# Last token group: row tables kept in the ring's tiles, token rows loaded between weights, and the experts' second bias added by VectorE

## The chip, the cores and the metric

The kernel runs on one core of a Trainium2 chip. The metric is the device time of one execution in microseconds (us). The kernel before was run three times: 3078.43, 3081.97 and 3084.2 us, median 3081.97. One more execution was taken with the hardware profiler; it took 3079.39 us.

Names of engines: PE is TensorE (PEld its weight loads), DVE is VectorE, ACT is ScalarE, POOL is GpSimd, SP is SyncE, which here only issues DMAs. SPq and POOLq are DMAs issued by those two.

## What is computed

One layer on a graph of 6250 nodes with 256 features and 206250 edges, sorted by destination, followed by a mixture of experts. Cut to what matters:

```
xn = layernorm(x)
# 1. attention over each node's edges, 8 heads of 32
sim  = (q[dst] * k[src]).sum(per head) / sqrt(32);  attn = softmax over the edges of one dst
agg  = segment_sum(attn * v[src], dst) @ Wo.T + bo
# 2. linear attention over all nodes, 8 heads of 64, with normalised k and v
mix  = (q @ (k.T @ v) / N) @ w_out.T + b_out
x    = x + agg + mix
# 3. mixture of experts: 8 experts, capacity C = ceil(1.25 * 6250 / 8)
h    = layernorm(x)
p    = softmax(h @ gate_w + gate_b);  idx = argmax(p)
buf[idx, pos] = h                      # pos: the token's place among those of its expert
y    = relu(buf[e] @ w1[e] + b1[e]) @ w2[e] + b2[e]
x    = x + y[idx, pos] * p[idx]        # dropped tokens (pos >= C) add nothing
```

All of it is in float32.

## The kernel before

**Blocks and groups.** The 6250 nodes make 49 blocks of 128 rows, one row in each partition of the on-chip memory. The nodes are ordered by their number of edges inside three groups of blocks, `GROUPS = (20, 17, 12)`, so that one block's nodes have nearly the same number of edges.

**Foreground: attention.** For each block the kernel runs over its edges in chunks of five, `W = 5`. POOL issues one indirect DMA per edge slot (L615) that gathers 128 key and value rows of 2 KB into a tile `kvg` of a ring of `RING = 11` tiles (pool `kvp`). For each chunk DVE multiplies the keys by the queries (L1353) and sums per head (L1354). When a unit (a block, or a part of one, some six chunks) has all its sums, ACT takes the exponentials, and during the next unit DVE multiplies the values by them (L1305) and PE adds them up with an identity matmul (L1309, into the PSUM tile `pa`). At the end of a unit DVE scales the sum into `ag` (L1327) and POOL scatters it to `agg_tab` (L823). POOL gathers at most `LEAD = 2` chunks ahead; a ring tile comes free when PE has read it at L1309.

**Background: everything else.** The order of all instructions is written out by the code, and each engine works through its own in that order. The other stages are Python generators. `background(n)` runs them for `n` units of estimated work, at two places within each chunk of attention: before `weigh` (L1305, L1309) and between `weigh` and the keys' products (L1353, L1354). So one chunk reads: a piece of background, L1305 and L1309, a piece of background, L1353 and L1354. When all blocks of group g have been scattered, the generator `behind(g)` is queued. It runs, in order:

- `output_stage`: for each block, load the aggregate, x transposed and x (L856, L199, L864), transpose the aggregate (L870, copied by ACT at L871), multiply by `weff` (L879) and `wo` (L888), add the two output biases by a matmul of `ones_d` and `bsum` (L891), add x (L897, L900), normalise (L902 to L916), write the sum to the DRAM table `x2_tab` (L917) and the normalised rows to `h_tab` (L918), and compute the gate's logits. Its steps s1 to s7 are pipelined over blocks.
- `routing`: the expert of each token, its place, the rows `row_to` and `row_from`, and the expert of each tile `tile_e`, on DVE.
- `to_tiles`: read `h_tab` again (L1087) and scatter the rows to `xbuf`, sorted by expert (L823).
- `experts`: tiles of 256 tokens in groups 0 and 1 (17 and 16 tiles), of 128 tokens in group 2 (19 tiles). Phase (0, t) is the first matmul of tile t (`hidden`, L1167, with relu on ACT at L1173), phase (1, t) the second (`final`, L1184, once per 128 tokens). Each phase loads one weight block of 1.0 to 1.2 MB, chosen by `tile_e` (L1132). The second bias is row 0 of a block of zeros behind the second weights: `final` adds it by a matmul with ones (L1188), ACT copies the result out of PSUM (L1190), SP writes it to `ybuf` (L1192). Token rows come in at L1142; that load waits for all scatters of its group.
- `finish`: gather each token's row from `ybuf` (L1227), read `x2_tab` (L1232), scale (L1244), add (L1248), write the output (L1249).

**The last group.** Groups 0 and 1 have the next group's attention to run beside. Group 2 has none: when its last aggregate is scattered, its stages run alone, from 2779 us to the end. Its weights go to the ring's tiles, which attention no longer needs, seven phases ahead (`AHEAD = 7`); the other groups have a pool of three tiles and load two ahead.

**SP's order.** SP issues its DMAs in the order of the code and stops at one whose wait isn't met. In the last group that order is: the output stage's loads and table writes, the reads of `h_tab` (each waits for a free buffer), seven weight loads, then the first two loads of token rows.

Of the kernel before, what the change touches and what calls it, by code (L numbers as in the profile page):

```python
# [9 lines left out]
F32 = mybir.dt.float32  # L10
# [3 lines left out]
ALU = mybir.AluOpType  # L14
# [4 lines left out]
P = 128  # L19
# [5 lines left out]
W = 5  # L25
RING = 11
LEAD = 2
PART = 44
GROUPS = (20, 17, 12)
# [39 lines left out]
def gps_layer(  # L69
# [59 lines left out]
    def rows(b):  # L129
        return tail if b == NB - 1 else P  # L130
# [21 lines left out]
    with tc.manual_schedule():  # L152
# [31 lines left out]
        bad = keep.tile([P, 3], F32, name="bad")  # L184
        flag_i = keep.tile([1, 1], I32, name="flag_i")
        bsum = keep.tile([P, D], F32, name="bsum")
        weff = keep.tile([P, DC, D], F32, name="weff")
        rstd = keep.tile([P, NB], F32, name="rstd")
        finite = keep.tile([P, NB], F32, name="finite")
# [494 lines left out]
        def linear_attention():  # L684
# [26 lines left out]
                )  # L711
                yield 2.4

            nc.vector.tensor_add(bsum, bias[:, 0, :], bias[:, 1, :])
            nc.vector.tensor_scalar(bsum, bsum, float(D) / P, None, op0=ALU.mult)
            wmf = wm.rearrange("p c g d -> p c (g d)")
            for c0 in range(0, 2 * MI, 512):
                less_mean(wmf[:, :, c0 : c0 + 512], 512)
# [127 lines left out]
        def output_stage(gi, logits):  # L846
# [2 lines left out]
            d2, d3 = late_pools["d2"], late_pools["d3"]  # L849
            wo, gw, gb = (late_pools[k] for k in ("wo", "gw", "gb"))  # L850
            T = {}

            def load(i):
                b = b0 + i
                ag = d2.tile([P, D], F32, name="in0")
                ld = nc.sync.dma_start(ag, agg_tab[b * P : (b + 1) * P, :])  # L856
                for s in sent["agg", gi]:
                    tc.add_manual_dep(ld.ins, s.ins.name, sync_data, reason="rows of any block")
                xT = d2.tile([P, D], F32, name="in1").rearrange("p (c q) -> p c q", c=DC)
                x_transposed(xT.rearrange("p c q -> p (c q)"), b)  # L860
                xb = d3.tile([P, D], F32, name="row_a")
                if rows(b) < P:
                    nc.vector.memset(xb, 0.0)
                nc.sync.dma_start(xb[: rows(b)], x[b * P : b * P + rows(b), :])  # L864
                T[i] = dict(ag=ag, xT=xT, xb=xb)

            def turn(t, to):
# [16 lines left out]
            def s2(i):  # L884
                t = T[i]
                po = t["po"]
                for c in range(DC):
                    nc.tensor.matmul(  # L888
                        po[:, 1, :], t["agT"][:, c, :], wo[:, c, :], start=False, stop=False, skip_group_check=True
                    )  # L890
                nc.tensor.matmul(po[:, 1, :], ones_d, bsum, start=False, stop=True, skip_group_check=True)  # L891

            def s3(i):
                t = T[i]
                x2 = d3.tile([P, D], F32, name="row_b")
                t["x2"] = x2
                nc.vector.scalar_tensor_tensor(  # L897
                    x2, t["po"][:, 0, :], rstd[:, b0 + i : b0 + i + 1], t["xb"], op0=ALU.mult, op1=ALU.add
                )
                nc.vector.tensor_add(x2, x2, t["po"][:, 1, :])  # L900
                st = d2.tile([P, 6], F32, name="std")
                nc.vector.bn_stats(st, x2)  # L902
                t["mv"] = d3.tile([P, 2], F32, name="mvd")
                nc.vector.bn_aggr(t["mv"], st)
                t["rs"] = d3.tile([P, 2], F32, name="rsd")
                nc.scalar.activation(t["rs"][:, 0:1], t["mv"][:, 1:2], AF.Sqrt, bias=eps)

            def s4(i):
                t = T[i]
                b = b0 + i  # L910
                rs = t["rs"]
                nc.vector.reciprocal(rs[:, 0:1], rs[:, 0:1])
                nc.vector.tensor_scalar(rs[:, 1:2], t["mv"][:, 0:1], rs[:, 0:1], -1.0, op0=ALU.mult, op1=ALU.mult)
                h = d3.tile([P, D], F32, name="hd")
                t["h"] = h
                nc.scalar.activation(h, t["x2"], AF.Identity, bias=rs[:, 1:2], scale=rs[:, 0:1])  # L916
                nc.sync.dma_start(x2_tab[b * P : (b + 1) * P, :], t["x2"])  # L917
                nc.sync.dma_start(h_tab[b * P : (b + 1) * P, :], h)  # L918

            def s5(i):  # L920
                t = T[i]
# [156 lines left out]
        def to_tiles(gi):  # L1078
            b0, ng = FIRST_OF[gi], GROUPS[gi]
            d3 = late_pools["d3"]  # L1080
            hs = {}

            def load(i):
                if i < ng:
                    b = b0 + i
                    hs[i] = d3.tile([P, D], F32, name="row_a")
                    nc.sync.dma_start(hs[i], h_tab[b * P : (b + 1) * P, :])  # L1087

            load(0)
            load(1)  # L1090
            yield 2.5
            for i in range(ng):
                load(i + 2)
                spaced_scatter(
                    ("x", gi), out=xbufs[gi][:, :],
                    out_offset=bass.IndirectOffsetOnAxis(ap=row_to[:, b0 + i : b0 + i + 1], axis=0),
                    in_=hs.pop(i), in_offset=None,
                )
                if i % 2:
                    yield 2.5  # L1100

        def experts(gi):
# [9 lines left out]
            for t in range(1, n_t):  # L1112
                phases += [(0, t), (1, t - 1)]
            phases.append((1, n_t - 1))
            AHEAD = 7 if last else 2

            def load_w(i):
                if i >= len(phases):
# [58 lines left out]
            def final(t, k, part):  # L1177
                w2_t = T[t][1]
                w = w2_t[:, :V2].rearrange("p (f d) -> p f d", f=FC)
                if part == 0:  # L1180
                    T[t]["py"] = bank((D,))
                py = T[t]["py"]
                for f in range(part * FC // 2, (part + 1) * FC // 2):
                    nc.tensor.matmul(  # L1184
                        py, T[t]["hT"][:, f, k * P : (k + 1) * P], w[:, f, :], start=(f == 0), stop=False
                    )
                if part == 1:
                    nc.tensor.matmul(py, ones[:, :P], w2_t[:, V2 : V2 + D], start=False, stop=True)  # L1188
                    yr = d2.tile([P, D], F32, name="res")
                    nc.scalar.copy(yr, py)  # L1190
                    r0 = t * size + k * P
                    nc.sync.dma_start(ybufs[gi][r0 : r0 + P, :], yr)  # L1192

            for i in range(AHEAD):
                load_w(i)
            load_x(0)
            load_x(1)
            yield 2.0
            turn(0)
            yield 1.0  # L1200
# [17 lines left out]
        def finish(gi):  # L1218
# [4 lines left out]
            def load(i):  # L1223
                if i < ng:
                    b = b0 + i
                    y = d3.tile([P, D], F32, name="row_a")
                    nc.gpsimd.indirect_dma_start(  # L1227
                        out=y, out_offset=None, in_=ybufs[gi][:, :],
                        in_offset=bass.IndirectOffsetOnAxis(ap=row_from[:, b : b + 1], axis=0),
                    )  # L1230
                    x2 = d3.tile([P, D], F32, name="row_b")
                    nc.sync.dma_start(x2, x2_tab[b * P : (b + 1) * P, :])  # L1232
                    T[i] = y, x2

            load(0)
# [706 lines left out]
```

## Time and profile before

| what | value |
|---|---|
| median of three runs | 3081.97 us |
| the profiled execution | 3079.39 us |
| its span, first to last instruction | 3077.6 us |
| PE busy | 2209.4 us, 72% |
| DVE busy | 2027.4 us, 66% |
| POOL busy | 1921.5 us, 62% |
| ACT busy | 640.9 us, 21% |
| DMA | 730.27 MB, mean 237 GB/s |
| gathers on POOL (L615) | 1715, the last at 2750.2 us |
| second matmuls, bias matmuls (L1188) | 85 tiles of 128 rows, two passes each |
| first and last bias matmul (L1188), groups 0 and 1 / group 2 | 1485.1 and 2681.7 / 2899.8 and 3034.2 us |
| last aggregate scatter | 2778.65 us |

The span is the time between the first and the last instruction of the profiled execution. Busy shares are means over stages with different limits, so the stretches have to be read one by one. A line of the timeline gives the start in us, the duration in us, the engine, the line of the kernel, the operation, what is written from what is read, the shape, and how many equal instructions were merged; in brackets stands how long the engine was idle before it and what it then waited for. A float32 matmul runs in two passes, so each matmul of the code stands twice.

### The profile page before, as it was taken

Reading aid. Unit: us, or ns where it says so; the run is one execution under the profiler, and the core shown is the slowest. Engines: PE = TensorE matmul, PEld = TensorE weight load, DVE = VectorE, ACT = ScalarE, POOL = GpSimd, SP = SyncE. Lnnn points to the kernel's source line nnn. Section 1 sums busy time; section 2 is a strip of 40 time slices with the busy share of each in tenths; the row PEclk is TensorE's granted clock in tenths of the full one; section 3 lists DMA queues with packets and bytes.
Section 4 is the critical chain, followed back from the end, with each engine's and each line's share of the span. In section 5 each row is a group of like instructions: output and inputs, shape, how many; then the busy total and the mean of one; then the engine's idle time right before and its main releaser. Section 6 shows DMA issues by size and latency. Waiting matters only on the chain. (4 is left out here: it accounts for less than half of the span.)

```text
span 3077.6 us, 29537 instructions
## 1 busy us (share of the span) xinstructions
PE 2209.4 (72%) x9086; PEld 1722.8 (56%) x9086; DVE 2027.4 (66%) x2723; ACT 640.9 (21%) x1802; POOL 1921.5 (62%) x2114
## 2 busy tenths in 40 slices
PE   8845468777777655763989889455628999846494
PEld 3534345555555444652778777334527888735494
DVE  6468778888888867983767776565854767564000
ACT  5200013333333101210211111101202222112242
POOL 5435767777777777667777777776466767650101
PEclk9977689899998778886999999678869999978797
DMA  7755957677777668867888887767658988763783
GB/s 263 274 189 179 335 169 215 208 210 212 208 210 219 200 196 251 264 194 230 304 287 308 292 302 246 227 202 248 203 182 276 316 303 311 244 191 110 281 326 110
DMA packets 291641, 730.27 MB, mean 237 GB/s; under 512 B 46838, under 2 KB 152020, under 8 KB 278164
## 3 DMA queue, kind: packets, MB, share of 16 engines
q0 software_dynamic: 149744, 477.83, 50.0%
q1 hardware_dynamic: 141732, 250.47, 23.1%
q8 instruction: 75, 1.23, 0.2%
q14 instruction: 90, 0.74, 0.1%
HBM read 654.47 MB, written 73.64 MB: 237 GB/s over the span
## 5 line engine op out<-in xcount | busy, mean ns | idle before, releaser
L615 POOL DMA_INDIRECT kvg<-kv_tab,idx x1715 | 1625.8, 948 | 668.2 <-issue 430.1
L1309 PE MATMUL pa<-kvg,ident 128*128 128x256 f32 x3430 | 1012.1, 452 | 586.3 <-DVE kvg L1305 453.4
L1309 PEld LDWEIGHTS pa<-kvg,ident 128*128 128x128 f32 x3430 | 756.9, 227 | 826.3 <-DVE kvg L1305 543.0
L1353 DVE TENSOR_TENSOR kvg<-kvg,qc 128x1280 f32<-128x1280 f32 (+1 forms) x366 | 512.9, 1402 | 397.5 <-DMA kvg<-kv_tab,idx 322.0
L1354 DVE TENSOR_REDUCE sim<-kvg 128x40 f32<-128x1280 f32 (+1 forms) x366 | 513.3, 1402 | 12.6
L1305 DVE TENSOR_TENSOR kvg<-kvg,pr 128x1280 f32<-128x1280 f32 (+1 forms) x366 | 509.6, 1393 | 0.0
L1184 PE MATMUL bank<-wt,hTe 128*128 128x256 f32 x1056 | 246.9, 381 | 0.0
L1167 PE MATMUL bank<-xTe,wt 128*128 128x256 f32 x1056 | 242.6, 381 | 2.3 <-ACT xTe L1157 2.3
L1167 PEld LDWEIGHTS bank<-xTe,wt 128*128 128x128 f32 x1056 | 201.6, 191 | 30.5 <-ACT xTe L1157 3.0
L1184 PEld LDWEIGHTS bank<-wt,hTe 128*128 128x128 f32 x1056 | 200.9, 192 | 27.0
L1248 DVE TENSOR_TENSOR res<-bank,row_b 128x256 f32<-128x256 f32 x49 | 20.7, 422 | 279.9 <-ACT bank L1244 271.7
L731 PE MATMUL bank<-wm,xTm 128*128 128x512 f32 x392 | 177.6, 596 | 0.0
L1227 POOL DMA_INDIRECT row_a<-ybuf,row_from x49 | 46.4, 947 | 197.3 <-issue 189.3
L1173 ACT ACTIVATE hTe<-bank,wt 128x256 f32<-128x256 f32 x264 | 110.8, 471 | 262.2 <-PE bank L1167 262.2
L1190 ACT COPY res<-bank 128x256 f32<-128x256 f32 x85 | 31.7, 372 | 439.5 <-PE bank L1188 248.0
L731 PEld LDWEIGHTS bank<-wm,xTm 128*128 128x128 f32 x392 | 72.0, 193 | 71.2 <-issue 70.9
L823 POOL DMA_INDIRECT xbuf<-row_a,row_to x49 | 48.0, 980 | 95.0 <-DVE cmp L1068 66.3
L1281 ACT COPY qc<-qs 128x256 f32<-128x256 f32 x49 | 18.8, 383 | 414.5 <-DVE kvg L1353 312.5
L823 POOL DMA_INDIRECT agg_tab<-ag,node_ri x49 | 48.5, 990 | 84.2 <-DVE ag L1327 61.5
L1153 PE MATMUL bank<-ident,in 128*128 128x128 f32 x170 | 29.0, 286 | 99.9 <-DMA in<-xbuf 99.9
L760 ACT ACTIVATE ck<-bank,rk 128x64 f32<-128x64 f32 x392 | 86.1, 339 | 50.3 <-DVE rk L757 50.2
L524 PE MATMUL pkv<-wn,xT 128*128 128x512 f32 x196 | 90.9, 618 | 2.7 <-DVE kv L538 2.6
(254 smaller groups left out, 2202.2 us busy)
## 6 DMA issues: line engine op xcount, KB each, us to landing
wt<-in_w_rows_dram SPq DMA_DIRECT2D x33, 1152.0 KB, 7.6
wt<-in_w_rows_dram SPq DMA_DIRECT2D x33, 1028.0 KB, 5.4
kvg<-kv_tab,idx POOLq DMA_INDIRECT x1715, 3.9
kvg<-in_w_rows_dram SPq DMA_DIRECT2D x19, 1152.0 KB, 13.2
kvg<-in_w_rows_dram SPq DMA_DIRECT2D x19, 1028.0 KB
kv_tab<-kv SPq DMA_DIRECT2D x49, 256.0 KB, 3.0
xT<-in_xT_all_dram SPq DMA_DIRECT2D x24, 512.0 KB, 6.7
in<-xbuf SPq DMA_DIRECT2D x85, 128.0 KB, 8.9
```

What stands on the lines that cost most here:

```text
L524: nc.tensor.matmul(pkvs[b], xTs[b // GX][:, b % GX, c, :], wn[:, c, : 2 * D], start=(c == 0), stop=(c == DC - 1))
L615: nc.gpsimd.indirect_dma_start(out=kv[:, j - j0, :], out_offset=None, in_=kv_tab[:, :], in_offset=bass.IndirectOffsetOnAxis(ap=idx_of[b][: ...
L731: nc.tensor.matmul(pm, xT_of[b][:, c, :], wmf[:, c, s * MI : (s + 1) * MI], start=(c == 0), stop=(c == DC - 1),)
L760: nc.scalar.activation(cks[b][:, h, :], pms[b][0][:, h * MD : (h + 1) * MD], AF.Copy, scale=rk[:, h : h + 1])
L823: s = nc.gpsimd.indirect_dma_start(**kw)
L1167: nc.tensor.matmul(ph[:, k, :], w[:, c, f * P : (f + 1) * P], T[t]["xT"][:, c, :size], start=(k == 0 and c == 0), stop=(k == 1 and c == DC ...
L1173: nc.scalar.activation(T[t]["hT"][:, f, :size], ph[:, k, :], AF.Relu, bias=w1_t[:, V1 + f : V1 + f + 1])
L1184: nc.tensor.matmul(py, T[t]["hT"][:, f, k * P : (k + 1) * P], w[:, f, :], start=(f == 0), stop=False)
L1305: nc.vector.tensor_tensor(vals, vals, v["pr"][:, j0 - s0 : j1 - s0, :, None].to_broadcast([P, m, GH, GD]), ALU.mult)
L1309: nc.tensor.matmul(v["pa"], ident, kv[:, j, D:], start=(j0 + j == s0), stop=(j0 + j == s1 - 1),)
L1353: nc.vector.tensor_tensor(keys, keys, qc[:, None, :].to_broadcast([P, j1 - j0, D]), ALU.mult)
L1354: nc.vector.tensor_reduce(sim[:, j0 - s0 : j1 - s0, :], keys.rearrange("p j (h d) -> p j h d", d=GD), AX.X, ALU.add)
```

## The change

There are four edits.

1. In the last group, the normalised rows `h` and the sums `x2` stay on chip: four tiles of the ring, two for each, hold the twelve blocks. The writes to `h_tab` and `x2_tab` and the reads from them are left out for this group. With four tiles taken, `AHEAD` becomes 11 - 4 - 2 = 5.
2. In the last group, the two output biases are added to the x rows by POOL (`bias_all`) instead of by a matmul with `ones_d`.
3. In `experts`, two weight blocks are loaded, then the first two loads of token rows, then the other weights. For groups 0 and 1, which load two ahead, the order is as it was.
4. In all three groups, the second bias is written into all 128 rows of its block, and DVE adds it while it takes the result out of PSUM. The matmul with ones and ACT's copy go. The blocks keep their size.

```diff
--- before.py
+++ after.py
@@ -184,6 +184,7 @@
         bad = keep.tile([P, 3], F32, name="bad")
         flag_i = keep.tile([1, 1], I32, name="flag_i")
         bsum = keep.tile([P, D], F32, name="bsum")
+        bias_all = keep.tile([P, D], F32, name="bias_all")
         weff = keep.tile([P, DC, D], F32, name="weff")
         rstd = keep.tile([P, NB], F32, name="rstd")
         finite = keep.tile([P, NB], F32, name="finite")
@@ -711,8 +712,8 @@
                 )
                 yield 2.4
 
-            nc.vector.tensor_add(bsum, bias[:, 0, :], bias[:, 1, :])
-            nc.vector.tensor_scalar(bsum, bsum, float(D) / P, None, op0=ALU.mult)
+            nc.vector.tensor_add(bias_all, bias[:, 0, :], bias[:, 1, :])
+            nc.vector.tensor_scalar(bsum, bias_all, float(D) / P, None, op0=ALU.mult)
             wmf = wm.rearrange("p c g d -> p c (g d)")
             for c0 in range(0, 2 * MI, 512):
                 less_mean(wmf[:, :, c0 : c0 + 512], 512)
@@ -849,6 +850,14 @@
             d2, d3 = late_pools["d2"], late_pools["d3"]
             wo, gw, gb = (late_pools[k] for k in ("wo", "gw", "gb"))
             T = {}
+            last = gi == NG - 1
+            if last:
+
+                R = 2 * W
+                for name in ("h", "x2"):
+                    ts = [kvp.tile([P, W, 2 * D], F32, name="kvg") for _ in range(-(-ng // R))]
+                    ts = [t.rearrange("p j (k d) -> p (j k) d", k=2) for t in ts]
+                    late_pools[name] = [ts[i // R][:, i % R, :] for i in range(ng)]
 
             def load(i):
                 b = b0 + i
@@ -862,6 +871,8 @@
                 if rows(b) < P:
                     nc.vector.memset(xb, 0.0)
                 nc.sync.dma_start(xb[: rows(b)], x[b * P : b * P + rows(b), :])
+                if last:
+                    nc.gpsimd.tensor_add(xb, xb, bias_all)
                 T[i] = dict(ag=ag, xT=xT, xb=xb)
 
             def turn(t, to):
@@ -886,13 +897,15 @@
                 po = t["po"]
                 for c in range(DC):
                     nc.tensor.matmul(
-                        po[:, 1, :], t["agT"][:, c, :], wo[:, c, :], start=False, stop=False, skip_group_check=True
-                    )
-                nc.tensor.matmul(po[:, 1, :], ones_d, bsum, start=False, stop=True, skip_group_check=True)
+                        po[:, 1, :], t["agT"][:, c, :], wo[:, c, :], start=False,
+                        stop=(last and c == DC - 1), skip_group_check=True,
+                    )
+                if not last:
+                    nc.tensor.matmul(po[:, 1, :], ones_d, bsum, start=False, stop=True, skip_group_check=True)
 
             def s3(i):
                 t = T[i]
-                x2 = d3.tile([P, D], F32, name="row_b")
+                x2 = late_pools["x2"][i] if last else d3.tile([P, D], F32, name="row_b")
                 t["x2"] = x2
                 nc.vector.scalar_tensor_tensor(
                     x2, t["po"][:, 0, :], rstd[:, b0 + i : b0 + i + 1], t["xb"], op0=ALU.mult, op1=ALU.add
@@ -911,11 +924,12 @@
                 rs = t["rs"]
                 nc.vector.reciprocal(rs[:, 0:1], rs[:, 0:1])
                 nc.vector.tensor_scalar(rs[:, 1:2], t["mv"][:, 0:1], rs[:, 0:1], -1.0, op0=ALU.mult, op1=ALU.mult)
-                h = d3.tile([P, D], F32, name="hd")
+                h = late_pools["h"][i] if last else d3.tile([P, D], F32, name="hd")
                 t["h"] = h
                 nc.scalar.activation(h, t["x2"], AF.Identity, bias=rs[:, 1:2], scale=rs[:, 0:1])
-                nc.sync.dma_start(x2_tab[b * P : (b + 1) * P, :], t["x2"])
-                nc.sync.dma_start(h_tab[b * P : (b + 1) * P, :], h)
+                if not last:
+                    nc.sync.dma_start(x2_tab[b * P : (b + 1) * P, :], t["x2"])
+                    nc.sync.dma_start(h_tab[b * P : (b + 1) * P, :], h)
 
             def s5(i):
                 t = T[i]
@@ -1081,7 +1095,9 @@
             hs = {}
 
             def load(i):
-                if i < ng:
+                if i < ng and gi == NG - 1:
+                    hs[i] = late_pools["h"][i]
+                elif i < ng:
                     b = b0 + i
                     hs[i] = d3.tile([P, D], F32, name="row_a")
                     nc.sync.dma_start(hs[i], h_tab[b * P : (b + 1) * P, :])
@@ -1112,7 +1128,7 @@
             for t in range(1, n_t):
                 phases += [(0, t), (1, t - 1)]
             phases.append((1, n_t - 1))
-            AHEAD = 7 if last else 2
+            AHEAD = RING - 2 * (-(-GROUPS[gi] // (2 * W))) - 2 if last else 2
 
             def load_w(i):
                 if i >= len(phases):
@@ -1182,19 +1198,20 @@
                 py = T[t]["py"]
                 for f in range(part * FC // 2, (part + 1) * FC // 2):
                     nc.tensor.matmul(
-                        py, T[t]["hT"][:, f, k * P : (k + 1) * P], w[:, f, :], start=(f == 0), stop=False
+                        py, T[t]["hT"][:, f, k * P : (k + 1) * P], w[:, f, :], start=(f == 0), stop=(f == FC - 1)
                     )
                 if part == 1:
-                    nc.tensor.matmul(py, ones[:, :P], w2_t[:, V2 : V2 + D], start=False, stop=True)
                     yr = d2.tile([P, D], F32, name="res")
-                    nc.scalar.copy(yr, py)
+                    nc.vector.tensor_add(yr, py, w2_t[:, V2 : V2 + D])
                     r0 = t * size + k * P
                     nc.sync.dma_start(ybufs[gi][r0 : r0 + P, :], yr)
 
-            for i in range(AHEAD):
-                load_w(i)
+            load_w(0)
+            load_w(1)
             load_x(0)
             load_x(1)
+            for i in range(2, AHEAD):
+                load_w(i)
             yield 2.0
             turn(0)
             yield 1.0
@@ -1228,8 +1245,11 @@
                         out=y, out_offset=None, in_=ybufs[gi][:, :],
                         in_offset=bass.IndirectOffsetOnAxis(ap=row_from[:, b : b + 1], axis=0),
                     )
-                    x2 = d3.tile([P, D], F32, name="row_b")
-                    nc.sync.dma_start(x2, x2_tab[b * P : (b + 1) * P, :])
+                    if gi == NG - 1:
+                        x2 = late_pools["x2"][i]
+                    else:
+                        x2 = d3.tile([P, D], F32, name="row_b")
+                        nc.sync.dma_start(x2, x2_tab[b * P : (b + 1) * P, :])
                     T[i] = y, x2
 
             load(0)
@@ -1889,8 +1909,7 @@
     w1_rows = np.concatenate(
         [w1.reshape(nx, d // P, P, f).transpose(0, 2, 1, 3).reshape(nx, P, -1), b1_t], axis=2
     ).reshape(nx * P, -1)
-    b2_rows = np.zeros((nx, P, d), np.float32)
-    b2_rows[:, 0] = b2
+    b2_rows = np.repeat(b2[:, None, :], P, axis=1)
     w2_rows = np.concatenate(
         [w2.reshape(nx, f // P, P, d).transpose(0, 2, 1, 3).reshape(nx, P, -1), b2_rows], axis=2
     ).reshape(nx * P, -1)
```

## The prediction

> **What bounds the kernel now.** I first read the busy time by slices, then the waits, then single stretches of the timeline, last the chain. The profiled execution took 3079.39 us, its span 3077.6; the 1.8 us outside are unchanged, and all sums are made on this execution, which lies 2.6 us under the median of 3081.97.
>
> The first view is busy time by stretch: the experts of group 0, those of group 1, the start of the latter, and the last group's steady state (PE, PEld, DVE, ACT, POOL busy; clock; DMA share; GB/s).
>
> ```profile
> 1480.00:1925.00 445.00, 401.86 (x1820) 344.97 (x1819) 313.08 (x287) 77.39 (x190) 334.80 (x363) 0.98 0.86 290
> 2300.00:2682.00 382.00, 358.06 (x1675) 313.07 (x1676) 239.59 (x226) 78.53 (x191) 262.89 (x286) 0.98 0.86 295
> ...
> 2300.00:2340.00 40.00, 23.17 (x101) 19.69 (x102) 14.32 (x18) 7.61 (x18) 21.34 (x25) 0.76 0.77 258
> ...
> 2930.00:2940.00 10.00, 10.00 (x71) 9.41 (x70) 0.00 (x0) 3.77 (x12) 0.00 (x0) 1.00 0.93 350
> ```
>
> Beside attention, PE is busy 402 of 445 us and, after a start with 16.8 us idle, nearly all of 382. POOL issues a gather each 1.25 us (0.95 and a 0.30 gap), so about 30.4 busy in 40 is its full rate: in group 0's stretch POOL paces (334.8 of 445), in group 1's PE does. From 2686 to 2750 POOL paces again. The last group runs alone after 2780, bound by PE.
>
> The waits show who stands for whose result (total us, times, longest):
>
> ```profile
> ACT res L1190 <- PE bank L1188: 248.0, 47, 9.0
> ...
> DVE row_b L897 <- PE bank L891: 58.3, 27, 12.5
> ```
>
> ACT, with time to spare, now waits for the experts' PSUM result. Where DVE waits for PE, it has stood up to 12.5 us. One tile's end, in the timeline:
>
> ```profile
> 2639.70 1.48 DVE L1353 TENSOR_TENSOR kvg<-kvg,qc 128x1280 f32<-128x1280 f32 x1
> ...
> 2641.22 1.49 DVE L1354 TENSOR_REDUCE sim<-kvg 128x40 f32<-128x1280 f32 x1
> ...
> 2642.62 1.48 DVE L1305 TENSOR_TENSOR kvg<-kvg,pr 128x1280 f32<-128x1280 f32 x1
> ...
> 2645.53 1.89 PE L1184 MATMUL bank<-wt,hTe 128*128 128x256 f32 x8
> ...
> 2647.26 0.59 PE L1188 MATMUL bank<-wt,ones 128*128 128x256 f32 x2
> ...
> 2647.93 0.37 ACT L1190 COPY res<-bank 128x256 f32<-128x256 f32 x1 [5.24 <-PE bank L1188]
> ...
> 2650.93 2.13 PEld L1309 LDWEIGHTS pa<-kvg,ident 128*128 128x128 f32 x10
> ```
>
> In the code's order this L1190 stands before the L1353 of 2639.70: DVE runs nearly 8 us ahead of PE there, and its L1305 (ready at 2644.10) is done 6.8 us before PE's L1309 asks. That lead is what keeps PE from waiting.
>
> The last group's chain, and its loop in the output stage:
>
> ```profile
> 2846.02 2.44 DMA xbuf<-row_a,row_to
> ...
> 2864.34 6.78 DMA xbuf<-row_a,row_to
> 2871.27 14.02 DMA in<-xbuf
> ```
> ```profile
> 2806.26 0.59 PE L891 MATMUL bank<-bsum,ones_d 128*128 128x256 f32 x2
> ...
> 2806.89 0.48 DVE L897 SCALAR_TENSOR_TENSOR row_b<-bank,rstd,row_a 128x256 f32<-128x256 f32 x1 [1.40 <-PE bank L891]
> ```
>
> The first token rows, behind seven weight loads, take 14.02 us; group 1's took 2.04. DVE's L897 waits for the bias matmul in every block.
>
> [...] DVE's 2723 records stand in the code's order. [...] the trace shows 429 from 2870 to 2875.
>
> **The change, part by part.**
>
> *Row tables in the ring.* Output stage: twelve bias matmuls leave a serial loop (L888, L891, L897 to L906, L871, L888), at 2 x 0.216 us: -5.2. The bias goes into the x rows on POOL. No POOL add is in the trace. [...] It lies between the x row's landing (about 2 us after issue) and L897: 2782.07 to 2787.59 for the first block, so 3.5 us of cover; POOL has nothing else there. I take 0; past the cover each us would cost up to 12. The 24 table writes, 24 reads and their SP issues lie beside the loop: 0. POOL's first scatter waits for row_to as before (2846.02), but four later ones waited 1.67, 1.49, 0.33 and 1.58 us for h rows where the others wait 0.19: -4.3. Four of the ring's eleven tiles go to the tables; hence the five weights ahead instead of seven.
>
> *Token rows first.* SP reaches the first weights when tile_e is ready (2846.7) instead of behind h loads (2862.6); two weights are in by 2854. The x loads then hold SP until the last scatter lands, and weights 2 to 4 queue behind them: not later than before, for the scatters end by 2863. From the last scatter's start to the first transpose took 2885.33 - 2864.34 = 21.0 us; now 2.44 landing, 0.4 issue, 2.04 landing: -16.1. Next late is the third tile's x load, behind four weights: counted from the first x issue, 0.9 us of issues, 2.0 to the first landing, 4.46 MB at 429 GB/s (10.4) and 0.3 of its own make 13.6; it is wanted after 2.04 + 10.7 = 12.7 (first to third transpose, 2885.33 to 2896.00): +0.9, bounds 0 and 4. The steady state prefetches five weights, 2.5 tiles or 18 us, enough for two loads.
>
> *Bias by DVE, last group.* 19 x 0.432 off PE: -8.2; the add (0.42) replaces a copy (0.37) on an idle DVE. The finish loses twelve x2 reads between its output writes (2.2 to 3.4 us each): -1.5, bounds -3 and 0. Tail: -5.2 - 4.3 - 16.1 + 0.9 - 8.2 - 1.5 = **-34.4**.
>
> *Bias by DVE, groups 0 and 1.* 66 adds go into DVE's queue among attention's products. An add waits for PE's L1184; behind it stand L1353, L1354 and L1305, or L1305 alone, and PE's next L1309 waits for that. In the example: L1184 ends at 2647.42; 0.06 to start, add 0.42, then 1.48 + 1.49 + 1.48 make 2652.35. PE, with L1188 gone, would reach L1309 at 2650.50: it waits 1.85 us. I set the records of both engines in the code's order and made the same sum at all 66 places (mean wait of PE):
>
> - group 0: 17 with L1305 alone, 2.09 each; 13 with three behind, 3.30; 4 at a node block's end, 2.88: 90.0 us
> - group 1: 12 x 1.65, 17 x 2.75, 3 x 3.31: 76.5 us
>
> It is positive in every one. PE's time in group 0's stretch becomes 401.9 - 34 x 0.432 + 90.0 = 477.2 against 445: +32, as PE's idle 43 us absorb the rest. In group 1's: 358.1 - 13.8 + 76.5 + 16.8 idle at the start = 437.6 against 382: +56. Nothing returns it later: POOL paces after both stretches, in order, and its gathers wait for ring slots that PE frees. Sum **+88**. Bounds: 35 (half of PE's waits fall where it waits anyway) and 138 (no idle absorbed). DVE's own 66 x 0.42 is inside. The rest of the move costs nothing by itself: the PSUM bank is freed by an engine that stands waiting for it, as ACT did (0.1 us after L1188), the y rows go out behind the add as they did behind the copy, and ACT loses waits that have spare time to hide in; only L1371 on ACT, for which DVE's L1375 waited 34.2 us in all, may come sooner, up to -10, which I leave to the range.
>
> Sum: 3079.4 - 34.4 + 88 = 3133.0.
>
> **Rivals.** (1) *The adds are hidden.* DVE is idle 132 and 142 us in the two stretches, so waits could fall into its waits for gathers. Against it: it is idle because it runs ahead, and the walk finds each L1305 too late. If it holds, the tail's gain and group 1's matmuls (-13.8, of which POOL lets some 12 through) give 3079.4 - 34.4 - 12 = 3033. It decides from a mean loss under 34.4/66 = 0.52 us per add, where I have 1.33. (2) *The last group starves for weights.* Demand rises from 2.49 MB in 7.68 us to 7.25, 344 GB/s; DMA share goes from 0.89 to 0.94 with two loads fewer ahead. If PE waits 0.8 us per tile, 19 x 0.8 = 15 more: 3148. For: the 0.93 above. Against: 429 GB/s was reached with weights alone. (3) *The tail's gain isn't there* (POOL's add on the loop, rows late): 3133 + 25 = 3158; against it speak the covers above.
>
> **Chances.** Forecast 0.62 (3095 to 3160), rival 1 0.12, rival 2 0.13, rival 3 0.08; 0.05 for an attention loss that just meets the gain. 0.2% is 6 us, about what a measurement can tell. Slower 0.84, same 0.03, faster 0.13. Range 3075 to 3165: below lie rival 1 and a little of the bound of 35 (3081), above part of rival 3 and of the bound of 138.
>
> **What would show it.** Right: DVE's new add waits for PE's L1184 over 150 us in total; PE's waits at L1309 for L1305 (453.4 us) grow by over 100; the last gather moves from 2750 to about 2838; from the last aggregate scatter (2778.65) to the end takes 265 us instead of 299; the first transpose comes 5 us after the last scatter; tiles take 7.25 us. Wrong, if PE's waits at L1309 hardly grow, or tiles in the last group stay at 7.68.

## The result: slower by 3.7%, and the profile after

The changed kernel takes 3194.18 us (median of four runs, 3189.86 to 3197.86) against 3081.7 for the kernel before (four runs, 3078.43 to 3084.2): a ratio of 1.0366, 95% interval 1.0353 to 1.038. The forecast was 3133, range 3075 to 3165: the sign was right, the size was not. The profiled execution has a span of 3195.0 us against 3077.6.

Where the time went can be cut at the last aggregate scatter, the end of attention. It starts at 2926.07 us, after 2778.65 before: 147.4 us later (forecast 88). From there to the end it is 268.7 us, after 298.7: 30.0 us less (forecast 34.4). (The end is taken at the last instruction that is no semaphore's, 0.2 us before the end of the span.) The tail did nearly what the sum said. Attention beside the experts of groups 0 and 1 lost 59 us more than the sum said.

Busy time by stretch of the changed kernel: the experts of group 0, those of group 1, and ten microseconds of the last group (columns as in the prediction: length; PE, PEld, DVE, ACT, POOL busy; clock; DMA share; GB/s).

```profile
1484.00:1996.00 512.00, 414.08 (x1744) 346.98 (x1742) 321.61 (x320) 65.24 (x156) 334.62 (x362) 0.92 0.77 254
2372.00:2830.00 458.00, 376.78 (x1610) 316.72 (x1610) 245.83 (x254) 67.30 (x160) 262.60 (x286) 0.92 0.73 246
3060.00:3070.00 10.00, 10.00 (x66) 9.28 (x65) 0.42 (x1) 3.65 (x12) 0.00 (x0) 1.00 0.97 364
```

PE is idle for 97.9 us in the first and 81.2 in the second. It is also busy for 414.08 and 376.78 us, though the bias matmuls are gone. Before, at a clock of 0.98, it was busy 401.86 and 358.06 with them. The clock is now 0.92 in both. The last row shows a PE without a gap at full clock, with a DMA share of 0.97.

The waits of the changed kernel (total us, times, longest), two of the kernel before, and from the page the adds of groups 0 and 1 alone (busy us, mean ns; idle before them):

```profile
PE pa L1329 <- DVE kvg L1325: 528.3, 197, 15.4
DVE res L1205 <- PE bank L1200: 492.0, 81, 36.7
POOL agg_tab L824 <- DVE ag L1347: 172.6, 21, 16.3
```
```profile
PE pa L1309 <- DVE kvg L1305: 453.4, 160, 16.0
POOL agg_tab L823 <- DVE ag L1327: 61.5, 13, 14.3
```
```profile
L1205 DVE TENSOR_TENSOR res<-bank,wt 128x256 f32<-128x256 f32 x66 | 28.0, 424 | 350.3 <-PE bank L1200 350.1
```

The new add is L1205; it stands 350.1 us for PE's second matmuls, L1200, in the two groups. PE's waits at L1329 (before: L1309) for DVE's weighing L1325 (before: L1305) grew from 453.4 to 528.3. The scatter of aggregates waits 172.6 us for DVE, after 61.5. ACT's 248.0 us of waiting at the old copy are gone; that gains nothing that can be measured (kernel 4 below keeps such a copy, with 220.0 us of waiting for PE, and is as fast as kernel 7, which has none).

One add in the timeline of the changed kernel (start, duration, engine, line, operation; in brackets the idle time before it and its releaser):

```profile
2597.90 2.32 PE L1329 MATMUL pa<-kvg,ident 128*128 128x256 f32 x10
...
2600.05 3.62 PE L1200 MATMUL bank<-wt,hTe 128*128 128x256 f32 x16
2601.98 0.42 DVE L1205 TENSOR_TENSOR res<-bank,wt 128x256 f32<-128x256 f32 x1 [9.13 <-PE bank L1200]
2602.32 1.48 DVE L1373 TENSOR_TENSOR kvg<-kvg,qc 128x1280 f32<-128x1280 f32 x1
2603.83 1.49 DVE L1374 TENSOR_REDUCE sim<-kvg 128x40 f32<-128x1280 f32 x1
2605.24 1.48 DVE L1325 TENSOR_TENSOR kvg<-kvg,pr 128x1280 f32<-128x1280 f32 x1
...
2606.77 4.64 PE L1329 MATMUL pa<-kvg,ident 128*128 128x256 f32 x10 [3.10 <-DVE kvg L1325]
```

DVE stands for 9.13 us, adds, and only then does three products that PE needs the last of. PE stands for 3.10 us. And the ten passes that took 2.32 us at 2597.90 take 4.64, just double, at 2606.77. The clock of these two stretches (columns as above):

```profile
2597.90:2600.22 2.32, 2.32 (x12) 2.06 (x11) 0.00 (x0) 0.00 (x0) 1.89 (x2) 1.00 0.99 361
2606.77:2611.41 4.64, 4.64 (x11) 3.75 (x12) 0.00 (x0) 0.00 (x0) 3.73 (x4) 0.50 0.69 203
```

This place shows both parts of the loss. The prediction had the 3.10 (its kind of place: 3.30 and 2.75 on average); it did not have the doubling.

The start of the last group's experts, in the timeline of the changed kernel:

```profile
3004.57 0.96 POOL L824 DMA_INDIRECT xbuf<-kvg,row_to  x1 [0.19 <-issue]
3007.29 0.81 SPq L1158 DMA_DIRECT2D in<-xbuf  x2
3009.36 0.69 PE L1169 MATMUL bank<-ident,in 128*128 128x128 f32 x2 [26.47 <-DMA in<-xbuf]
...
3016.66 0.38 PE L1169 MATMUL bank<-ident,in 128*128 128x128 f32 x2
...
3023.65 0.41 PE L1169 MATMUL bank<-ident,in 128*128 128x128 f32 x2 [2.01 <-DMA in<-xbuf]
```

The first transposes come 4.8 us after the last scatter's start (forecast 4.9). Before, it was 21.0: the scatter of 2864.34 in the prediction's chain, and this line:

```profile
2885.33 0.69 PE L1153 MATMUL bank<-ident,in 128*128 128x128 f32 x2 [46.59 <-DMA in<-xbuf]
```

The third tile's rows make PE wait 2.01 us.

### The profile page after: what moved, and what is told of

It is laid out like the page before. It is cut to its first block, busy times and chain, and to the rows that moved or that the text cites. A ratio compares the mean times of both kernels' runs of the same rounds, so it can differ in the third digit from the quotient of the medians.

```text
span 3195.0 us, 29068 instructions
## 1 busy us (share of the span) xinstructions
PE 2236.7 (70%) x8892; PEld 1724.8 (54%) x8892; DVE 2056.4 (64%) x2808; ACT 609.0 (19%) x1717; POOL 1928.8 (60%) x2126
## 5 line engine op out<-in xcount | busy, mean ns | idle before, releaser
L1329 PE MATMUL pa<-kvg,ident 128*128 128x256 f32 x3430 | 1060.5, 468 | 696.3 <-DVE kvg L1325 528.3
L1329 PEld LDWEIGHTS pa<-kvg,ident 128*128 128x128 f32 x3430 | 781.4, 235 | 960.6 <-DVE kvg L1325 631.1
L1325 DVE TENSOR_TENSOR kvg<-kvg,pr 128x1280 f32<-128x1280 f32 (+1 forms) x366 | 509.3, 1392 | 0.0
L1205 DVE TENSOR_TENSOR res<-bank,wt 128x256 f32<-128x256 f32 x66 | 28.0, 424 | 350.3 <-PE bank L1200 350.1
L1200 PE MATMUL bank<-wt,hTe 128*128 128x256 f32 x1056 | 247.1, 385 | 0.0
L1200 PEld LDWEIGHTS bank<-wt,hTe 128*128 128x128 f32 x1056 | 204.9, 196 | 29.1
L824 POOL DMA_INDIRECT agg_tab<-ag,node_ri x49 | 48.0, 979 | 191.6 <-DVE ag L1347 172.6
L1205 DVE TENSOR_TENSOR res<-bank,kvg 128x256 f32<-128x256 f32 x19 | 8.1, 424 | 155.5 <-PE bank L1200 141.8
L741 ACT ACTIVATE sq<-bank 128x512 f32<-128x512 f32 x98 | 56.5, 593 | 161.7 <-PE bank L732 161.7
```

The lines of the kernel that those rows point to most:

```text
L741: nc.scalar.activation(sqs[b][:, s * MH : (s + 1) * MH, :].rearrange("p g d -> p (g d)"), pms[b][s], AF.Square)
L1200: nc.tensor.matmul(py, T[t]["hT"][:, f, k * P : (k + 1) * P], w[:, f, :], start=(f == 0), stop=(f == FC - 1))
L1325: nc.vector.tensor_tensor(vals, vals, v["pr"][:, j0 - s0 : j1 - s0, :, None].to_broadcast([P, m, GH, GD]), ALU.mult)
L1329: nc.tensor.matmul(v["pa"], ident, kv[:, j, D:], start=(j0 + j == s0), stop=(j0 + j == s1 - 1),)
```

## Experiments

The theory, formed from the two traces: each add of groups 0 and 1 stops DVE behind PE, PE then waits for DVE, and besides, these waits lower the clock that PE is granted, so that its own work takes longer. Rivals: the loss comes from another edit (the tables in the ring); it is DVE's own 28 us of adds; the wait would only move elsewhere; the longer matmuls have nothing to do with the waits.

All runs in one table. "Attention" is the start of the last aggregate scatter, "tail" the time from there to the end, both in the profiled execution. "Half" is time at half speed (a granted clock of 0.50) in groups 0 / 1: the sum of the trace's half-speed clock records that begin between the first matmul of a group's experts and the last. Each ratio is to runs of the kernel before in the same comparison; their medians lie between 3078.94 and 3081.7.

| kernel | median us | ratio to before, 95% interval | attention | tail | half |
|---|---|---|---|---|---|
| before | 3081.7 | | 2778.7 | 298.7 | 20.5 / 0 |
| changed | 3194.18 | 1.0366 (1.0353 to 1.038) | 2926.1 | 268.7 | 81.9 / 58.0 |
| 1 tail's edits only | 3050.60 | 0.9906 (0.9889 to 0.9922) | 2780.6 | 267.3 | 20.5 / 0 |
| 2 adds of groups 0, 1 only | 3226.92 | 1.0479 (1.0461 to 1.0496) | 2916.1 | 301.6 | 75.1 / 54.6 |
| 3 adds in group 0, not 1 | 3116.28 | 1.0114 (1.0097 to 1.0131) | 2847.0 | 270.1 | 81.9 / 0 |
| 4 no bias in groups 0, 1 | 3034.23 | 0.9856 (0.9839 to 0.9872) | 2762.7 | 267.9 | 34.1 / 0 |
| 5 three fillers | 3148.93 | 1.0227 (1.021 to 1.0244) | 2872.7 | 267.3 | 13.7 / 10.2 |
| 6 six fillers | 3170.40 | 1.0294 (1.0277 to 1.0311) | 2901.9 | 267.2 | 17.1 / 6.8 |
| 7 adds held back | 3031.57 | 0.9849 (0.9833 to 0.9866) | 2756.6 | 269.1 | 27.3 / 0 |
| 8 tail, weights first | 3052.18 | 0.9915 (0.9898 to 0.9931) | 2775.1 | 268.7 | 23.9 / 0 |
| 9 tail, output bias by PE | 3055.35 | 0.9923 (0.9906 to 0.9939) | 2776.3 | 274.5 | 20.5 / 0 |
| 10 tail, second bias by PE | 3055.14 | 0.9923 (0.9907 to 0.994) | 2771.9 | 275.5 | 20.5 / 0 |
| 11 tables only | 3063.00 | 0.9948 (0.9932 to 0.9965) | 2777.4 | 281.4 | 23.9 / 0 |
| 12 order only | 3080.12 | 1.0000 (0.9989 to 1.0011) | 2777.3 | 297.0 | 17.1 / 0 |

The end of attention varies between kernels whose attention is the same (2771.9 to 2780.6 in kernels 1, 8, 9, 10), so for edits of a few microseconds the tail is the better measure. It varies too: from 267.2 to 270.1 in the changed kernel and kernels 1 and 3 to 7, whose tails are the same.

### Which edit loses the time (kernels 1, 2, 3)

Kernel 1, from the changed kernel; `ones_p` is a 128 x 128 tile of 1/128, so that the matmul over 128 equal rows gives the bias once. The `stop` of the matmul ahead of it moves with it (not shown). In kernel 3 the tuple is `(1,)`. Kernel 2 makes the opposite edit in the kernel before, with the 128 bias rows filled.

```diff
-                    nc.vector.tensor_add(yr, py, w2_t[:, V2 : V2 + D])
+                    if gi in (0, 1):
+                        nc.tensor.matmul(py, ones_p, w2_t[:, V2 : V2 + D], start=False, stop=True)
+                        nc.scalar.copy(yr, py)
+                    else:
+                        nc.vector.tensor_add(yr, py, w2_t[:, V2 : V2 + D])
```

> The changed kernel, but in groups 0 and 1 the experts' second bias is again a matmul and ScalarE's copy; only the last group's adds are VectorE's. Theory (the whole loss sits in the 66 adds of groups 0 and 1, which stop VectorE behind TensorE): attention's last gather is back at 2750 and the tail keeps its 30 us (298.95 to 268.9 from the last aggregate scatter to the end), so 3081.7 - 30 = 3052, between 3045 and 3060. Rival (the row tables in the ring's tiles, or the other edits, disturb the groups before): above 3080.

> The kernel before, with one edit alone: in groups 0 and 1 VectorE adds the second bias from PSUM; the last group and its tail are as before. Theory: the last aggregate scatter is 143 to 148 us later as in the changed kernel, the tail stays at 299: 3081.7 + 147 = 3229, between 3220 and 3235. Rival (the adds cost my forecast of 88, the rest comes from other edits): 3170.

> The changed kernel with VectorE's adds in group 0 and in the last; group 1 has TensorE's bias matmuls and ScalarE's copies again. Theory (each group pays for its own adds): 3050.6 + 65 = 3116, between 3108 and 3122; group 0's half-speed stretches as in the changed kernel (some 80 us), none in group 1. Rival (group 1's loss is what group 0 leaves behind, through gathers and the ring): 3150 or more.

Measured: 3050.60, 3226.92 and 3116.28 us against 3052, 3229 and 3116. The adds of the two groups alone cost 147.6 us against the kernel before in the same comparison (3079.31), the rest of the change gives 28.7. Together that is 118.9 us, where the whole change costs 112.5 (3194.18 - 3081.7): they add up within 6.4 us. Group 0's adds cost 65.7 (3116.28 - 3050.60) and group 1's 77.9 (3194.18 - 3116.28), between kernels of different comparisons. Tables, order and the tail's biases disturb nothing ahead of them. Kernel 3's two groups in one profile:

```profile
1459.00:1991.00 532.00, 437.94 (x1850) 368.41 (x1851) 333.22 (x328) 72.52 (x173) 351.81 (x382) 0.92 0.76 257
2388.00:2750.00 362.00, 353.35 (x1661) 309.75 (x1660) 235.13 (x220) 77.75 (x190) 255.08 (x276) 1.00 0.86 296
```

With the adds the clock is 0.92, without them 1.00, in the same execution. Group 0's loss leaves nothing behind for group 1.

### Is it the stand or the work (kernels 4 and 7)

Kernel 7 keeps all 66 adds on DVE, but issues each behind the next weighing of values; the weight load that takes the add's tile is held back with it. The last lines stand in `weigh`; `release` issues what is held. Kernel 4 leaves the second bias of groups 0 and 1 out.

```diff
+                    def add():
+                        yr = d2.tile([P, D], F32, name="res")
+                        nc.vector.tensor_add(yr, py, w2_t[:, V2 : V2 + D])
+                        r0 = t * size + k * P
+                        nc.sync.dma_start(ybufs[gi][r0 : r0 + P, :], yr)
+
+                    if last:
+                        add()
+                    else:
+                        held.append(add)
...
-                load_w(i + AHEAD)
+                if held:
+                    held.append(lambda j=i + AHEAD: load_w(j))
+                else:
+                    load_w(i + AHEAD)
...
                 nc.tensor.matmul(
                     v["pa"], ident, kv[:, j, D:], start=(j0 + j == s0), stop=(j0 + j == s1 - 1),
                 )
+            release()
```

> The changed kernel, but in groups 0 and 1 each add is held back and issued behind the next weighing of attention's values, with the weight load that takes its tile. The same adds, 66 of 0.42 us, are still VectorE's. Theory (the cost is VectorE's stand behind TensorE just ahead of a weighing, not the adds' own 28 us): TensorE no longer waits, its granted clock is back near 0.98 in both groups, and the 66 matmuls of some 0.2 us are saved: 3052 - 13 = 3039, between 3030 and 3060. Rival 1 (the wait only moves to the next weighing): 3100 to 3160. Rival 2 (VectorE's own busy time is what counts): 3052 + 28 = 3080.

> The changed kernel, but groups 0 and 1 leave the second bias out: ScalarE copies the result, with neither the matmul nor the add. The part of the computation left out is that bias. Theory: 66 matmuls of 0.216 us come off TensorE where it is the bound, so some 13 us below the kernel that has them, 3039; a bound from below for any way of adding the bias elsewhere. Rival (TensorE's bias matmuls were already in its idle time): 3052, no gain.

Measured: 3031.57 and 3034.23 us. The same adds, one weighing later, cost nothing that can be measured beside no bias at all, and the kernel is 162.6 us below the changed one and 1.5% below the kernel before. In its profile the adds of groups 0 and 1, and the two groups:

```profile
L1212 DVE TENSOR_TENSOR res<-bank,wt 128x256 f32<-128x256 f32 x66 | 27.8, 422 | 79.3 <-PE bank L1206 79.2
```
```profile
1456.00:1918.00 462.00, 415.07 (x1849) 353.92 (x1850) 337.68 (x330) 72.86 (x173) 351.06 (x380) 0.97 0.87 294
2315.00:2661.00 346.00, 339.23 (x1596) 296.73 (x1594) 245.22 (x250) 67.08 (x159) 254.66 (x276) 1.00 0.88 308
```

DVE still does 27.8 us of adds, but stands 79.2 us for PE instead of 350.1, and at a place where the next weighing is already done. Both rivals, that the wait moves and that DVE's own time counts, fall. One of the 66 in the timeline of kernel 7 (L1341 is the weighing, L1345 its sum on PE):

```profile
2578.85 3.62 PE L1206 MATMUL bank<-wt,hTe 128*128 128x256 f32 x16
2579.48 1.48 DVE L1341 TENSOR_TENSOR kvg<-kvg,pr 128x1280 f32<-128x1280 f32 x1
2580.88 0.42 DVE L1212 TENSOR_TENSOR res<-bank,wt 128x256 f32<-128x256 f32 x1
...
2582.30 2.32 PE L1345 MATMUL pa<-kvg,ident 128*128 128x256 f32 x10
```

PE goes from the second matmul into attention's sum without a stop. Against kernel 1, kernels 4 and 7 save 16.4 and 19.0 us; I had expected 13. I had counted one pass per bias matmul there, and there are two of 0.216 us each (ten passes at L1309 take 2.32 us, eight take 1.89), 28.5 us in all; about 60% of it came through.

### Does the clock matter by itself (kernels 5 and 6)

From the changed kernel, in groups 0 and 1, with n = 3 and n = 6:

```diff
                     nc.sync.dma_start(ybufs[gi][r0 : r0 + P, :], yr)
+                    if not last:
+                        pf = bank((D,))
+                        for j in range(n):
+                            nc.tensor.matmul(pf, ident, wo[:, 0, :], start=(j == 0), stop=(j == n - 1))
```

> The changed kernel with three matmuls more behind each of the 66 final parts of groups 0 and 1, on the output projection's weights into a bank of their own that nobody reads (some 1.2 us of TensorE each, 79 us in all, at the 0.2 us per pass of the other matmuls). They fall where TensorE stands waiting for VectorE. Theory (some 60 of the 147 us are the lower granted clock, called forth by the waits): TensorE has 79 us more to do, and the kernel is yet faster, as the half-speed stretches go: 3194 - 45 = 3150, between 3135 and 3170, at a granted clock of 0.95 or more in the two groups. Rival (the longer matmuls aren't the waits' doing, or the clock is no cause): 3194 to 3205.

> As the kernel with three, with six such matmuls at each of the 66 places: 158 us more of TensorE's work, about as much as its gaps over 1 us hold in the two groups (93 and 65 us). Theory: the clock is full in both groups, and what is over of the fillers costs: 3149, between 3130 and 3175, 20 to 70 us below the changed kernel in spite of 158 us more work. Rival: 3194 to 3270, since what doesn't fall into a gap is added.

Measured: 3148.93 and 3170.40 us, 45.3 and 23.8 below the changed kernel, with 198 and 396 matmuls more for PE. The groups with three fillers, then with six:

```profile
1455.00:1958.00 503.00, 451.80 (x2049) 384.73 (x2049) 333.63 (x328) 72.43 (x172) 352.11 (x383) 0.98 0.81 272
2354.00:2777.00 423.00, 388.92 (x1784) 333.57 (x1783) 241.47 (x248) 66.81 (x159) 254.76 (x276) 0.99 0.75 253
```
```profile
1459.00:1972.00 513.00, 492.66 (x2248) 426.80 (x2249) 332.38 (x327) 72.24 (x173) 352.11 (x382) 0.98 0.79 266
2368.00:2806.00 438.00, 424.25 (x1964) 369.01 (x1963) 241.55 (x248) 66.70 (x159) 254.63 (x276) 0.99 0.72 244
```

The clock is back at 0.98 and 0.99. Kernel 5, which does useless work in PE's gaps, is faster by those 45.3 us than the changed kernel, which lets PE stand, so part of the loss is the clock's, and the gaps bring it on. DVE's adds still stand 446.5 us for PE in kernel 5 (all groups; 492.0 in the changed kernel), so the two losses come apart: with the clock nearly whole, attention ends 94.1 us later than before, where the sum without a term for the clock said 88. What the fillers themselves cost is in the 94.1 and isn't known apart. With six, PE is busy 492.66 of 513 us and 424.25 of 438, and the two stretches are 10 and 15 us longer than with three: the fillers no longer fit and begin to cost. The time is 21 us above the 3149 that I expected, within the range.

### The tail, edit by edit (kernels 8 to 12)

Kernel 8 is kernel 1 with edit 3 undone; kernel 9 is kernel 1 with edit 2 undone; kernel 10 is kernel 1 with the tuple `(0, 1, 2)`. Kernel 11 is the kernel before with edit 1 alone, kernel 12 the kernel before with edit 3 alone. The core of 8, and of 12:

```diff
-            load_w(0)
-            load_w(1)
+            for i in range(AHEAD):
+                load_w(i)
             load_x(0)
             load_x(1)
-            for i in range(2, AHEAD):
-                load_w(i)
```
```diff
-            for i in range(AHEAD):
-                load_w(i)
+            load_w(0)
+            load_w(1)
             load_x(0)
             load_x(1)
+            for i in range(2, AHEAD):
+                load_w(i)
```

> The kernel with the tail's edits only, but in the last group all five weights are issued ahead of the first two tiles' token rows, as before the change. Theory (the row loads wait for the last token scatter, so the weights behind them in SyncE's queue start only then, and the third tile's rows stand behind them): with the weights first, they land while the scatters run, the first transposes stay 4.8 us after the last scatter's start, and the 2 to 3 us stall ahead of the third tile's transposes is gone: 3050.6 - 3 = 3048, tail 264. Rival (the first rows stand behind three weights more, as my forecast's -16.1 us for this edit has it): tail 267 + 10 = 277, 3061.

> The kernel with the tail's edits only, but the last group's output stage adds its two biases by a matmul on TensorE again, instead of GpSimd's add on the x rows. Theory (my term of 12 x 0.432 us, nothing lost to GpSimd's add): tail 267.3 + 5.2 = 272.5, 3050.6 + 5 = 3056. Rival (GpSimd's add of 0.72 us is late in each block and gives the gain back): tail 267 or less, 3050.

> The kernel with the tail's edits only, but in the last group, too, the experts' second bias is a matmul and ScalarE's copy. Theory (19 x 0.432 us on TensorE, which bounds these tiles): tiles take 7.68 us again, tail 267.3 + 8.2 = 275.5, 3059. Rival (the tiles are bound by the weights' transfers at 7.25): tail 267, 3051.

> The kernel before with edit 1 alone: the last group's row tables in the ring's tiles, five weights ahead, in the order of before, all biases by TensorE. Theory (SyncE is free of the reads of the normalised rows, so the five weights are issued some 20 us earlier and are in by the last scatter): the first transposes come some 9 us after the last scatter's start instead of 21, tail 298.7 - 4.3 (scatters) - 12 - 1 = 281.5, 3062. Rival (the gain at the first rows is the new order's, edit 3): tail 294, 3075.

> The kernel before with edit 3 alone: in the last group two weights, then the first two tiles' token rows, then five weights; the row tables in DRAM as before. Theory (each of edits 1 and 3 takes the weights out of the way of the first rows by itself): the first transposes come some 8 to 10 us after the last scatter's start instead of 21, the third tile's rows wait 2 to 4 us behind five weights: tail 289, 3069. Rival (without the tables the two weights ahead are still under way, and the weights behind the rows are late for the third tile): tail 298, 3079.

Undoing the second bias's move costs the tail 8.2 us (275.5 against 267.3), as 19 x 0.432 has it; tiles take 7.68 us again. Undoing the output bias's move costs 7.2, where 5.2 was expected, a difference within the spread of the tails. The tables alone give 17.3 us of tail (281.4 against 298.7).

The order of edit 3 is the surprise. Undone (kernel 8), it costs the tail 1.4 us; done alone (kernel 12), it gives 1.7, both within the spread of the tails, and the time is the same as before. The timeline of kernel 12:

```profile
2869.99 0.81 SPq L1142 DMA_DIRECT2D in<-xbuf  x2
2871.94 0.69 PE L1153 MATMUL bank<-ident,in 128*128 128x128 f32 x2 [34.52 <-DMA in<-xbuf]
2876.35 0.68 SPq L1142 DMA_DIRECT2D in<-xbuf  x1
2878.92 0.38 PE L1153 MATMUL bank<-ident,in 128*128 128x128 f32 x2
2891.27 0.66 PE L1153 MATMUL bank<-ident,in 128*128 128x128 f32 x2 [7.37 <-DMA in<-xbuf]
```

The first transposes come 8.9 us after the last scatter's start instead of 21.0, as expected. But the third tile's rows, issued at 2876.35 behind five weights, keep PE waiting for 7.37 us at 2891.27. I had expected 2 to 4 there, and a gain of 10; my rival was right. In kernel 8 the expected 3 us were not found either: the third tile no longer waits, but the first transposes come 8.9 us after the last scatter's start instead of 4.6. What makes the row loads early is chiefly edit 1: without the reads of the normalised rows SP issues the first weights 65.1 us after the last aggregate scatter in kernel 8 and 68.7 in kernel 11, instead of 84.0 before; I take it that less of them is then still under way when the rows are wanted.

## Why the prediction was wrong, step by step

**The tail, -34.4 forecast, -30.0 measured: the sum right, its largest term only in part for its reason.** Scatters -4.3: they run without gaps, 18.3 us from the first to the last before, 13.9 after. First rows -16.1: measured -16.2 (21.0 to 4.8 us). But I put that gain under the new order. The tables alone bring 11.9 of it (first transposes 9.1 us after the last scatter in kernel 11); the order alone brings 12.1 (kernel 12) and loses it again at the third tile. That the term came out to 0.1 us is luck. Third tile +0.9, bounds 0 and 4: first to third transposes took 14.3 us instead of 10.8, +3.5; 2.0 of it is the wait for rows, 1.3 a first tile that took 7.3 us instead of 6.0 (mean clock 0.58 there, after 0.73). Experts -8.2: tiles take 7.25 us instead of 7.68, as forecast. Finish -1.5: from the last matmul of the experts to the end 40.8 us instead of 42.8, so -2.0. Output stage -5.2: the first scatter comes 64.6 us after the last aggregate scatter instead of 67.4, so -2.8; with the edit undone it comes at 69.2, with it at 64.2 (kernels 9 and 1), so single profiles spread by some 2 us here. A block of the loop takes 3.50 us (from one L910 to the next) instead of 3.86 (L897), 0.36 less where 0.432 was forecast. GpSimd's add, for whose time the trace of the kernel before held no figure, takes 0.72 us and is hidden in eleven of twelve blocks, but not in the last one, whose x row landed late:

```profile
2972.76 0.72 POOL L875 TENSOR_TENSOR row_a<-row_a,bias_all 128x256 f32<-128x256 f32 x1 [9.09 <-DMA row_a<-in_x_dram]
2973.51 0.48 DVE L910 SCALAR_TENSOR_TENSOR kvg<-bank,rstd,row_a 128x256 f32<-128x256 f32 x1 [1.57 <-POOL row_a L875]
```

**PE's waits beside attention: right.** The step put PE's idle time at 90.0 us in group 0's stretch and at 76.5 + 16.8 in group 1's, 183.3 in all. The windows above show 97.9 and 81.2, together 179.1; errors of +7.9 and -12.1 cancel in part. The walk over 66 places, each with DVE's queue behind the add, holds where it was made: in the trace, PE's next L1329 behind an add's weighing waits at 65 of the 66 places, for 92.3 us in group 0 (forecast 90.0) and 70.9 in group 1 (76.5). It is what made the sign right.

**PE's own work: the step that failed.** In "PE's time in group 0's stretch becomes 401.9 - 34 x 0.432 + 90.0 = 477.2" and in its like for group 1, the busy time of the kernel before was carried over as it was, less the bias matmuls: 387.2 + 344.3 = 731.5 us. Measured: 414.08 + 376.78 = 790.9, which is 59.4 more, as much as the sum "+88" lacks to 147.4 (PE's idle time came out 4.2 lower, and some 4 us lie outside these stretches). It is not more work: kernel 7, with the same matmuls, is busy 415.07 and 339.23 us where the changed kernel, in windows of the same kind (first to last matmul of the group's experts), is busy 438.64 and 370.69. It is the clock. Half speed was granted for 81.9 us instead of 20.5 in group 0 and for 58.0 instead of 0 in group 1. Half of the 119.4 us more is lost, an estimate of 59.7.

The ground for it was in what I had read. The prediction's row for the start of group 1's stretch shows a PE with 16.8 us idle in 40 at a clock of 0.76. I used its idle time and passed over the clock beside it (though PE had stood 35.1 us for its rows there, far longer than at an add). My sum had waits of 1.7 to 3.3 us and no term for the clock. I laid PE's gaps beside the clock records of the changed kernel in the two groups: each of the 32 half-speed records begins inside a gap of PE or at most 1.4 us after its end. Of the 44 gaps of 1.7 to 3.4 us, 27 brought one on, that of the add shown above among them, and 17 did not; no run here tested what sets the two sorts apart.

**The bounds and rivals.** The bound of 138 for the adds was no bound, since it let every idle microsecond count but no change of PE's speed. Rival 1 (hidden) fell: DVE's new waits are long and PE's follow. Its time of 3033 is what kernel 7 reaches, by another order. Rival 2 (the weights starve the last group) fell: tiles take 7.25 us with a DMA share of 0.97, and behind the third tile PE never waits. Rival 3 (no gain in the tail) fell: 30.0 us of it are there.

**What I said would show it.** The new add waits over 150 us: 350.1. PE's waits at the weighing grow by over 100: those that the profile puts down to DVE grew by 74.9; PE's whole idle time in the two stretches grew by 112.0 (67.1 to 179.1), and 27.3 of it stands at the same line without a named releaser (24.2 to 51.5). The last gather at 2838: 2898.9. The tail at 265: 268.7. First transposes after 5 us: 4.8. Tiles of 7.25: 7.25.

## What to carry to other kernels

When an add or a copy moves to an engine that feeds the bound engine, look at what stands behind it in that engine's queue, and issue it where its input is already there: one weighing later made 162.6 us of difference here, with the same instructions. A wait of 3.10 us on TensorE cost twice here, once as idle time and once in the clock of what followed (ten passes took 4.64 us instead of 2.32), so a sum for such a stretch needs a line for the clock. And when two edits aim at the same stall, cost each alone and both together: of the tables and the new order, the tables alone gave 17.3 us of the tail, and the order beside them nothing that can be measured.

## What the runs showed of the hardware

Useless matmuls in TensorE's gaps made the changed kernel faster: 198 of them took 45.3 us off. In the changed kernel TensorE was granted half speed for 81.9 and 58.0 us in groups 0 and 1, with those matmuls for 13.7 and 10.2. One row load behind five weight loads in SyncE's queue came in 7.4 us after PE had stopped for it.
